# A gated recurrence: half B's state products as sums of three bf16 numbers, the x side with stationary weights, r in 64-column products

## The chip, the cores and the metric

The kernel runs on one core of a Trainium2 chip. The metric is device time in microseconds of one execution, as the median of the runs; lower is better. The engines are named as in the profile: PE is TensorE (matmuls; its weight loads are PEld), DVE is VectorE, ACT is ScalarE, POOL is GpSimd, SP is SyncE, whose queue issues most DMAs.

## What is computed

```python
xT = jnp.swapaxes(x, 0, 1)               # x: (8, 512, 512) = batch, time, units
def step(h, x_t):
    fused = jax.nn.sigmoid(jnp.concatenate([x_t, h], axis=-1) @ w_W + w_b)
    hidden_state, output_state = jnp.split(fused, 2, axis=-1)
    memory_state = x_t @ wx_W + wx_b + hidden_state * (h @ wh_W + wh_b)
    h_new = output_state * h + (1.0 - output_state) * jnp.tanh(memory_state)
    return (h_new, h_new)
_, hs = jax.lax.scan(step, h0, xT)
return x + jnp.swapaxes(hs, 0, 1)
```

There are 512 steps, each of which needs the state h (8 rows of 512 units) that the step before left. All numbers are fp32. In the kernel's names, r is `hidden_state`, z is `output_state`, "hh" (the h of the code's `turn_h`) is `h @ wh_W + wh_b`. The products with x_t (the x side) depend on no state and can be made ahead; those with h are on the recurrence.

## The kernel before

The 512 units are split in four quarters of 128. The state lies transposed, units on partitions: quarters 0 and 1 are half A (tiles `hTA`), 2 and 3 half B (`hTB`). A product takes a quarter of the state as the stationary operand (128 x 32: 8 columns of this step, the rest left from others) and 128 columns of a weight matrix as the moving one. Four such products, one for each j, write to the four column groups of 32 PSUM partitions (`mm` with `32 * j`, lines 177 and 273 to 275).

A group of `GS` = 4 steps shares its PSUM banks: R (r, all units), G (hh and z of half A) and H (z and hh of half B), two of each. The x side of a group is made one group ahead into a bank `xp` (`prefill`, lines 215 to 225: 384 moving columns, one quarter of x in each step), on top of a bias that ScalarE puts there (`seed`); ScalarE copies its parts into R, G and H (`spread`), so that the state's products add to them. VectorE transposes the x part of the tanh's argument (`turn_x`).

The order of PE's work is written out by hand (line 27), followed by one quarter of the x side:

```python
ORDER = "R0 R1 G0 G1 R2 R3 G2 G3 H0 H1 H2 H3"
```

R0 to G1 need half A of the new state; R2 to G3 need half B; so do H2 and H3. All engines run their instructions in the order of the program (`manual_schedule`, line 170), and that is, in a step (lines 351 to 372):

- `turn_r(0)`, `turn_r(1)`: VectorE transposes R's two halves (line 303), ScalarE takes the sigmoid (line 205).
- `turn_h(0)`, `turn_z(0)`: VectorE transposes hh and z of half A out of G (lines 321, 303), ScalarE takes the sigmoid of -z.
- `memory(0)`: a scan on VectorE makes r * hh + x side (lines 283, 342), ScalarE the tanh. `update(0)`: a scan makes the new state of half A (line 347).
- The same for half B out of H; its scans are in two pieces, one for each quarter.
- ScalarE copies both halves of the state into another slot; then `turn_x`, `spread` or `seed`, and three small memsets on VectorE.

GpSimd adds x to the new state (line 385) and the sync queue stores 16 steps at a time (line 395) and loads x two to three blocks ahead (line 101).

Of the kernel before, what the change touches and what calls it, by code (L numbers as in the profile page):

```python
# [10 lines left out]
ALU = mybir.AluOpType  # L11
PSUM = bass.MemoryType.PSUM
# [3 lines left out]
GS = 4  # L16
B = 8
HU = 64

DVE_FILL = 23
IDLE = 3
LAST = 4
SYNC = mybir.DependencyInfo(mybir.DependencyClass.Sync, mybir.DependencyReason.DATA)

ORDER = "R0 R1 G0 G1 R2 R3 G2 G3 H0 H1 H2 H3"

FIRST = "Q0 x Q1 x Q2 x Q3 H0 H1 H2 H3"

BANKS = ("R", "G", "H")

XP = {"G": slice(0, 128), "R": slice(128, 256), "X": slice(256, 384), "H": slice(384, 512)}
# [3 lines left out]
def tile_cond_rnn_residual(  # L37
# [5 lines left out]
    wgr_d: bass.AP,  # L43
    whh_d: bass.AP,
    wh3_d: bass.AP,
    bias_d: bass.AP,
    out: bass.AP,
# [8 lines left out]

# [3 lines left out]
    NG = T // GS  # L80
# [6 lines left out]

    xins = {}


    NX = NQ * TC * B // 2
    head = const.tile([P, NX + NQ * B], F32, name="head")
    nc.scalar.dma_start(out=head, in_=xh)
    hin = head[:, NX:].rearrange("p (k b) -> p k b", k=NQ)

    def load_x(c, half=slice(0, 2)):

        if c < NCH:
            if c not in xins:
                xins[c] = xin_p.tile([P, 2, NQ, TC * B // 2], F32, tag="xin", name=f"xin_{c}")  # L100
            nc.sync.dma_start(
                out=xins[c][:, half], in_=x[c].rearrange("p (e k n) -> p e k n", e=2, k=NQ)[:, half]
            )

    def x_of(c, k, t, n):

        e, t = divmod(t, TC // 2)
        if c == 0 and e == 0:
            first = head[:, :NX].rearrange("p (k n) -> p k n", k=NQ)
            return first[:, k, t * B : (t + n) * B]  # L110
        return xins[c][:, e, k, t * B : (t + n) * B]


    rows4 = const.tile([P, 512], F32, name="rows4")
    nc.vector.memset(rows4, 0.0)
    nc.scalar.dma_start(out=rows4[0:128:32], in_=bias_d)

    wx = const.tile([P, NQ, NQ, 384], F32, name="wx")
    for k in range(NQ):
        nc.sync.dma_start(out=wx[:, k], in_=wx_d[k])  # L120

    wgr = const.tile([P, NQ, NQ, 256], F32, name="wgr")
    for k in range(NQ):
        nc.sync.dma_start(out=wgr[:, k], in_=wgr_d[k])  # L124
    whh = const.tile([P, NQ, NQ, 128], F32, name="whh")
    nc.sync.dma_start(out=whh[:, :3], in_=whh_d)
    nc.sync.dma_start(out=whh[:, 3], in_=wh3_d)

    def wh(bank, k, j):
        return whh[:, k, j] if bank == "H" else wgr[:, k, j, {"G": slice(0, 128), "R": slice(128, 256), "Q": slice(0, 256)}[bank]]  # L130

    load_x(0, 1)

    def pair(n, name, rows, slots):

        if n == "A":
            return const.tile([P, rows, 2, slots], F32, name=name)
        return const.tile([P, 2, rows, slots], F32, name=name).rearrange("p c n s -> p n c s")

    NH = 2 * GS
    hT = [[pair(n, f"hT{n}{i}", 32, 3) for i in range(NH)] for n in "AB"]

    md0 = [[pair(n, f"md0{n}{i}", 32, 2) for i in range(2)] for n in "AB"]
    md1 = [[pair(n, f"md1{n}{i}", 32, 2) for i in range(2)] for n in "AB"]
    hd0 = [[pair(n, f"hd0{n}{i}", B, 3) for i in range(2)] for n in "AB"]
    zeros = const.tile([P, 512], F32, name="zeros")
    nc.vector.memset(zeros, 0.0)
    none = const.tile([P, 128], BF16, name="none")  # L150
    nc.vector.memset(none, 0.0)

    ones = const.tile([P, NQ, 32], F32, name="ones")
    nc.vector.memset(ones, 0.0)
    for j in range(NQ):
        nc.vector.memset(ones[32 * j : 32 * j + 1, j], 1.0)

    nc.scalar.activation(const.tile([P, 1], F32, name="table"), zeros[:, :1], AF.Sigmoid)
    for n, t_ in enumerate(hd0[0] + hd0[1] + md0[0] + md0[1] + hT[0] + hT[1]):
        (nc.vector if n < DVE_FILL else nc.gpsimd).memset(t_, 0.0)  # L160
    for t_ in hd0[0] + hd0[1]:
        nc.gpsimd.memset(t_[:, :, :, 1], -1.0)
    idle = const.tile([P, IDLE], F32, name="idle")

    def state(hf, i, slot=2):

        s = i % GS
        return hT[hf][i % NH][:, B * s : B * s + B, :, slot]

    ctx.enter_context(tc.manual_schedule())  # L170
    banks = [
        {n: psum.tile([P, 128], F32, name=f"{n}{q}") for n in BANKS}
        for q in range(2)
    ]
    xps = [psum.tile([P, 512], F32, name=f"xp{q}") for q in range(2)]

    def mm(out_, lhsT, rhs, start=False):
        nc.tensor.matmul(  # L178
            out_, lhsT, rhs, start=start, stop=False, skip_group_check=True
        )  # L180


    for t_ in list(banks[0].values()) + list(banks[1].values()):
        mm(t_, none[:, :128], none, start=True)
    def warm():

        mm(xps[1], zeros[:, :128], zeros)

    mm(xps[1], zeros[:, :128], zeros, start=True)
    warm()  # L190
    mm(xps[0], ones.rearrange("p j m -> p (j m)"), rows4, start=True)
    bias = const.tile([P, 512], F32, name="bias")
    nc.vector.tensor_copy(bias, xps[0])
    for hf in range(2):
        for slot in (0, 2):
            nc.vector.tensor_copy(
                state(hf, 0, slot), hin[:, 2 * hf : 2 * hf + 2].rearrange("p c b -> p b c")
            )

    written = {}

    def act(key, out_, in_, func, **kw):
        inst = nc.scalar.activation(out_, in_, func, **kw).ins  # L205
        if key in written:
            tc.declare_no_dep(inst, written[key], reason="ordered through VectorE")
        written[key] = inst
        return inst

    def seed(g):

        nc.scalar.copy(xps[g % 2], bias)

    def prefill(g):

        c, t0 = divmod(g * GS, TC)
        for k in range(NQ):
            for j in range(NQ):
                mm(  # L220
                    xps[g % 2][32 * j : 32 * j + 32, 64:448],
                    x_of(c, k, t0, GS),
                    wx[:, k, j, :],
                )
            yield

    def spread(g, names):

        for n in names:
            nc.scalar.copy(banks[g % 2][n], xps[g % 2][:, XP[n]])  # L230

    def turn_x(g, e):

        c0 = XP["X"].start + 32 * e
        nc.vector.transpose(
            md1[e // 2][g % 2][:, :, e % 2, 1], xps[g % 2][:, c0 : c0 + 32]
        )

    def take(it, n=None):
        while n is None or n > 0:  # L240
            if next(it, it) is it:
                return
            n = None if n is None else n - 1

    def x_side():
        for g in range(1, NG):
            yield from prefill(g)

    seed(1)
    take(prefill(0))  # L250
    warm()
    later = x_side()
    spread(0, "RGH")
    for e in range(NQ):
        turn_x(0, e)

    pool_done = {}
    for i in range(T):
        g, s = divmod(i, GS)
        c, t = divmod(i, TC)  # L260
        ps = banks[g % 2]
        if t == 0 and c > 0:
            load_x(c + 3)
        if t == 0:
            ot = out_p.tile([P, TC, NQ, B], F32, tag="ot", name=f"ot_{c}")

        for n in (ORDER if i else FIRST).split():
            if n == "x":
                take(later, 1)
                continue  # L270
            bank, k = n[0], int(n[1])
            hs = hT[k // 2][i % NH][:, :, k % 2, 2]
            for j in range(NQ):
                to = xps[0][:, :256] if bank == "Q" else ps[bank]
                mm(to[32 * j : 32 * j + 32, :], hs, wh(bank, k, j))
        take(later, 1)

        rows = slice(B * s, B * s + B)

        def scans(hf, out_, d0, d1):  # L280

            for c_ in [slice(0, 2)] if hf == 0 else [slice(0, 1), slice(1, 2)]:
                nc.vector.tensor_tensor_scan(  # L283
                    *[t_[:, :, c_].rearrange("p n c s -> p (n c s)") for t_ in (out_, d0, d1)],
                    0.0,
                    ALU.mult,
                    ALU.add,
                )
                yield c_

        if i:
            pg, pr = ps["G"], ps["R"]
        else:
            pg, pr = (xps[0][:, XP[n]] for n in "GR")
        raw = {
            "h": (pg[:, :HU], ps["H"][:, HU:]),
            "z": (pg[:, HU:], ps["H"][:, :HU]),
            "r": (pr[:, :HU], pr[:, HU:]),
        }

        def turned(n, hf):
            t_ = work.tile([P, 2, 32], F32, tag=f"t{n}{hf}", name=f"t{n}{hf}_{i}")
            inst = nc.vector.transpose(t_.rearrange("p c n -> p (c n)"), raw[n][hf]).ins  # L303
            return t_[:, :, rows], inst

        r_done = [None, None]

        def turn_r(hf):
            tr, inst = turned("r", hf)

            if hf == 1 and i + 1 - NH in pool_done:
# [170 lines left out]
```

## Time and profile before

| What | us |
|---|---|
| median of 3 runs (lowest, highest) | 1693.87 (1693.63, 1693.88) |
| span of the profiled execution | 1691.7 |
| what lies around the span, by the median | 2.2 |
| PE busy, DVE busy, ACT busy, POOL busy | 1680.3, 1087.0, 915.5, 231.2 |
| granted TensorE clock, mean | 1.000 |

The span runs from the first to the last instruction. In the groups, a line gives the line of the code, the engine, the operation, what it writes and reads, partitions x elements, how often, its busy time and the mean length of one, then the idle time ahead of it and what ended that. A matmul in fp32 appears as two instructions, each with a weight load. A matmul's end is modelled and includes the way through the array, so lengths of matmuls overlap; the chain shows by how much the next one is later. In the timeline, lines give start, length, engine and what ran, with the wait before it in brackets.

### The profile page before, as it was taken

The numbers are of one execution on the slowest core, as the hardware profiler recorded it, in microseconds if no ns is written. First come the engines' busy times: TensorE is split into PE (matmuls) and PEld (weight loads), VectorE is DVE, ScalarE is ACT, GpSimd is POOL, SyncE is SP. The second block draws the span as 40 slices with busy tenths as digits, with TensorE's granted clock in tenths as the row PEclk, the third lists the DMA queues.
The fourth block names the chain that finished last, engine by engine and source line by source line (L and its number), as shares of the span: only waits on it lengthen the run. The fifth ranks groups of instructions, "written<-read, shape, count | busy, mean of one in ns | idle before, by whom it ended". The sixth has DMA issues, their size and how long they took to land.

```text
span 1691.7 us, 121258 instructions
## 1 busy us (share of the span) xinstructions
PE 1680.3 (99%) x53230; PEld 1467.6 (87%) x53230; DVE 1087.0 (64%) x8229; ACT 915.5 (54%) x5121; POOL 231.2 (14%) x1032
## 2 busy tenths in 40 slices
PE   8999999999999999999999999999999999999998
PEld 6888888888888888888888888888888888888887
DVE  5666666666666666666666666666666666666666
ACT  3555555555555555555555555555555555555554
POOL 0111111111111111111111111111111111111111
PEclk9999999999999999999999999999999999999999
DMA  4000000000000000000000000000000000000000
GB/s 177 17 17 5 17 17 17 17 4 17 17 17 17 4 17 17 17 17 13 9 18 17 17 17 4 17 17 17 17 5 17 17 17 17 4 17 11 11 11 10
DMA packets 11483, 30.86 MB, mean 18 GB/s; under 512 B 1220, under 2 KB 1732, under 8 KB 10952
## 3 DMA queue, kind: packets, MB, share of 16 engines
q1 hardware_dynamic: 10800, 22.94, 3.9%
q8 instruction: 416, 6.82, 1.7%
q14 instruction: 115, 0.94, 0.2%
q10 hardware_dynamic: 152, 0.16, 0.0%
HBM read 14.70 MB, written 8.39 MB: 14 GB/s over the span
## 4 chain that ended last, share of the span: by engine, by line
PE 98%; DMA 1%; DVE 0%; ACT 0%; issue 0%; SPq 0%
PE R L178 26%; PE G L178 26%; PE H L178 26%; PE xp L178 19%; DMA whh<-in_whh_dram 1%; DMA head<-in_xh_dram 0%; DVE md1A L321 0%; DVE hTA L283 0%; ACT hd0A L205 0%; ACT hTA L205 0%; SPq L124 0%; DVE tz L303 0%; ACT hTB L205 0%; DVE hTB L283 0%; ACT hd0B L205 0%
## 5 line engine op out<-in xcount | busy, mean ns | idle before, releaser
L178 PE MATMUL xp<-wx,xin 128*32 128x384 f32 x4032 | 431.3, 486 | 0.0
L178 PEld LDWEIGHTS R<-wgr,hTA 128*32 128x32 f32 x8176 | 247.4, 135 | 206.8 <-DVE hTA L283 206.4
L303 DVE STREAM_TRANSPOSE tr<-R 128x64 f32<-128x64 f32 x1022 | 194.4, 229 | 309.1 <-PE R L178 309.1
L178 PE MATMUL R<-wgr,hTA 128*32 128x128 f32 x8176 | 330.9, 273 | 2.2 <-DVE hTA L283 2.2
L178 PE MATMUL H<-whh,hTA 128*32 128x128 f32 x8192 | 331.3, 273 | 0.8 <-DMA whh<-in_whh_dram 0.8
L178 PE MATMUL H<-whh,hTB 128*32 128x128 f32 x8192 | 331.2, 273 | 0.0
L178 PE MATMUL R<-wgr,hTB 128*32 128x128 f32 x8176 | 330.6, 273 | 0.0
L178 PE MATMUL G<-wgr,hTB 128*32 128x128 f32 x8176 | 330.6, 273 | 0.0
L178 PE MATMUL G<-wgr,hTA 128*32 128x128 f32 x8176 | 330.6, 273 | 0.0
L385 POOL TENSOR_TENSOR ot<-xin,hTB 128x16 f32<-128x16 f32 x503 | 126.4, 251 | 1415.6 <-DVE hTB L283 1324.0
L205 ACT ACTIVATE hd0B<-tz 128x16 f32<-128x16 f32 x512 | 114.9, 224 | 305.3 <-DVE tz L303 305.3
L205 ACT ACTIVATE md0A<-tr 128x16 f32<-128x16 f32 x512 | 119.6, 234 | 265.2 <-DVE tr L303 265.2
L178 PEld LDWEIGHTS H<-whh,hTA 128*32 128x32 f32 x8192 | 260.2, 136 | 1.2 <-DMA whh<-in_whh_dram 1.2
L178 PEld LDWEIGHTS G<-wgr,hTA 128*32 128x32 f32 x8176 | 259.8, 136 | 0.0
L178 PEld LDWEIGHTS H<-whh,hTB 128*32 128x32 f32 x8192 | 254.5, 122 | 0.0
L178 PEld LDWEIGHTS G<-wgr,hTB 128*32 128x32 f32 x8176 | 254.1, 122 | 0.0
L178 PEld LDWEIGHTS R<-wgr,hTB 128*32 128x32 f32 x8176 | 245.2, 122 | 0.0
L283 DVE TENSOR_TENSOR_SCAN hTA<-hd0A,hTA 128x48 f32<-128x48 f32 x512 | 132.1, 258 | 149.2 <-ACT hTA L205 149.2
L283 DVE TENSOR_TENSOR_SCAN hTB<-hd0B,hTB 128x24 f32<-128x24 f32 x1024 | 158.1, 196 | 104.0 <-ACT hTB L205 104.0
L205 ACT ACTIVATE hd0A<-tz 128x16 f32<-128x16 f32 x512 | 118.9, 232 | 111.4 <-DVE tz L303 111.4
L321 DVE STREAM_TRANSPOSE md1A<-G 128x64 f32<-128x64 f32 x511 | 156.8, 307 | 28.7
L205 ACT ACTIVATE hTB<-hTB 128x16 f32<-128x16 f32 x512 | 121.2, 237 | 81.1 <-DVE hTB L283 80.5
(62 smaller groups left out, 1680.2 us busy)
## 6 DMA issues: line engine op xcount, KB each, us to landing
xin<-in_x_dram SPq DMA_DIRECT2D x31, 256.0 KB, 3.8
out_dram<-ot SPq DMA_DIRECT2D x31, 256.0 KB, 3.3
wx<-in_wx_dram SPq DMA_DIRECT2D x4, 768.0 KB, 7.2
wgr<-in_wgr_dram SPq DMA_DIRECT2D x4, 512.0 KB, 9.7
whh<-in_whh_dram SPq DMA_DIRECT2D x1, 768.0 KB
whh<-in_wh_dram SPq DMA_DIRECT2D x1, 256.0 KB, 11.2
out_dram<-ot SPq DMA_DIRECT2D x1, 192.0 KB, 1.9
head<-in_xh_dram ACTq DMA_DIRECT2D x1, 144.0 KB, 5.2
```

The lines of the kernel that those rows point to most:

```text
L178: nc.tensor.matmul(out_, lhsT, rhs, start=start, stop=False, skip_group_check=True)
L205: inst = nc.scalar.activation(out_, in_, func, **kw).ins
L283: nc.vector.tensor_tensor_scan(*[t_[:, :, c_].rearrange("p n c s -> p (n c s)") for t_ in (out_, d0, d1)], 0.0, ALU.mult, ALU.add,)
L303: inst = nc.vector.transpose(t_.rearrange("p c n -> p (c n)"), raw[n][hf]).ins
L321: nc.vector.transpose(md1[hf][g % 2][:, :, :, 0].rearrange("p n c -> p c n"), raw["h"][hf])
L385: return engine.tensor_tensor(ot[:, t, 2 * hf : 2 * hf + 2, :].rearrange("p c n -> p n c"), x_of(c, slice(2 * hf, 2 * hf + 2), t, 1).rearr ...
```

## The change

- **Half B's hh and z.** Each fp32 number of the state and of the weights is written as an exact sum of three bf16 numbers. The weights' parts are made once at the start (`split_weights`: two ScalarE copies and two VectorE subtractions for each quarter). The state's parts are made in every step by two subtractions on VectorE for each half (`split`); each takes the upper 16 bits of a number as the bf16 part and leaves the rest in the next slot. The 24 stationary columns are 3 parts x 8 rows, so that each of 4 quarters x 3 weight parts x 4 column groups gives one bf16 product of 128 columns, into bank B. The nine part products (3 in columns, 3 in accumulation) are summed by the accumulation in PSUM and by what follows on VectorE: the memory scan runs over 5 slots (3 parts, bias or r, x side) and not 2, and z's slots are summed by a `tensor_reduce`.
- **r** is made in two banks, rA and rB, by fp32 products of 64 columns; hh and z of half A stay in G. The stationary operand has 8 columns, and the banks hold one step.
- **The x side** is made for 8 steps at once: the weights are stationary (128 x 32), x moves (64 columns), so that the results come with units on partitions. ScalarE brings each of 12 regions for 8 steps to SBUF with its bias (`leave`, in place of `seed` and `spread`). GpSimd adds the x side to the transposed r of both halves and to z of half A before the sigmoid (`gate`). Block 0 is made whole ahead of step 0.
- VectorE's order in a step: r of A, hh of A, z of A, memory scan of A, r of B, update of A, hh and z of B, the two subtractions for A, memory scan of B, reduction, update of B, the two subtractions for B. The idle memsets and `turn_x` go.
- The last block is stored in one piece, and its adds are all on GpSimd.

```diff
-ORDER = "R0 R1 G0 G1 R2 R3 G2 G3 H0 H1 H2 H3"
+ORDER = "rA01 G01 rB01 rA23 G23 rB23 B01 B23 x x x x x x"
...
+    def split(hf, i):
+        for part in range(2):
+            V.tensor_tensor(
+                state(hf, i, 2, part + 1), state(hf, i, 2, part), upper(hf, i, part), ALU.subtract
+            )
...
+    def split_weights(k):
+        S.copy(wb3[:, k, 0], halves(wb[:, k]))
+        V.tensor_tensor(rest[:, k], wb[:, k], wb3[:, k, 0], ALU.subtract)
+        S.copy(wb3[:, k, 1], halves(rest[:, k]))
+        V.tensor_tensor(wb3[:, k, 2], rest[:, k], wb3[:, k, 1], ALU.subtract)
...
+    def x_region(n, blk, g, c):
+        ch, t0 = divmod(blk * BS, TC)
+        to = xps[n % 3]
         for k in range(NQ):
             for j in range(NQ):
                 mm(
-                    xps[g % 2][32 * j : 32 * j + 32, 64:448],
-                    x_of(c, k, t0, GS),
-                    wx[:, k, j, :],
+                    to[32 * j : 32 * j + 32],
+                    wx[:, k, GATES.index(g), c, 32 * j : 32 * j + 32],
+                    x_of(ch, k, t0, BS),
+                    start=k == 0,
                 )
...
+    def leave(n, blk, g, c):
...
+        S.activation(to, of, AF.Identity, bias=biases[:, i : i + 1])
...
+    later = x_side()
+    for _ in range(12 * NQ):
+        next(later)
+        leave_all()
+    for k in range(NQ):
+        split_weights(k)
+    pieces = {"rA": ("rA", 0, 64), "rB": ("rB", 64, 64), "G": ("G", 128, 128)}
+    def products(i, name, k):
+        hs = st[k // 2][i % NS]
+        c = k % 2
+        if name == "B":
+            flat = top(hs).rearrange("p q b c s -> p (q b c s)")
+            lhsT = flat[:, 6 * c + 5 : 6 * c + 5 + 12 * 23 + 1 : 12]
+            for part in range(3):
+                for j in range(NQ):
+                    mm(bank["B"][32 * j : 32 * j + 24], lhsT, wb3[:, k, part, j], start=k + part == 0)
+            return
+        n, c0, w = pieces[name]
+        lhsT = hs[:, 0, :, c, 2]
+        for j in range(NQ):
+            mm(bank[n][32 * j : 32 * j + B, :w], lhsT, wf[:, k, j, c0 : c0 + w], start=k == 0)
...
+        def gate(name, hf, of, xs, to, key, **kw):
+            p_ = work.tile([P, 2, B], F32, tag=f"p{name}{hf}", name=f"p{name}{hf}_{i}")
+            G.tensor_tensor(p_, turned(name, hf, of), xs, ALU.add)
+            return act(key, to.rearrange("p b c -> p c b"), p_, AF.Sigmoid, **kw)
...
         turn_r(0)
-        turn_r(1)
-        turn_h(0)
-        turn_z(0)
+        V.transpose(
+            md1a[q][:, B * t : B * t + 32, :, 0].rearrange("p n c -> p c n"), bank["G"][:, :HU]
+        )
+        gate("z", 0, bank["G"][:, HU:], xz[q][:, :, rows], hd0[0][i % 2][:, :, :, 2], ("zc", 0, i % 2), scale=-1.0)
         memory(0)
+        turn_r(1)
         update(0)
-        turn_h(1)
-        turn_z(1)
-        memory(1)
-        update(1)
+        V.transpose(
+            md1b[q][:, rows, :, :4].rearrange("p b c s -> p c s b"), bank["B"][:, :HU]
+        )
+        V.transpose(zb[q][:, t, :, :4].rearrange("p c s b -> p c (s b)"), bank["B"][:, HU:])
+        act(("h", 0, (i + 1) % NS), state(0, i + 1, 0), state(0, i + 1), AF.Copy)
+        split(0, i + 1)
+        memory(1)
+        pz = work.tile([P, 2, B], F32, tag="pzB", name=f"pzB_{i}")
+        V.tensor_reduce(pz, zb[q][:, t].rearrange("p c s b -> p c b s"), AX.X, ALU.add)
+        act(("zc", 1, i % 2), hd0[1][i % 2][:, :, :, 2].rearrange("p b c -> p c b"), pz, AF.Sigmoid, scale=-1.0)
+        update(1)
+        act(("h", 1, (i + 1) % NS), state(1, i + 1, 0), state(1, i + 1), AF.Copy)
+        split(1, i + 1)
+        leave_all()
```

## The prediction

> **What bounds the kernel now.** I read the page first (busy line and chain by engine), then the chain in order of time, then the groups by form, then the timeline of one steady step.
>
> ```profile
> PE 1680.3 (99%) x53230; PEld 1467.6 (87%) x53230; DVE 1087.0 (64%) x8229; ACT 915.5 (54%) x5121; POOL 231.2 (14%) x1032
> ...
> PE 98%; DMA 1%; DVE 0%; ACT 0%; issue 0%; SPq 0%
> ```
>
> TensorE is busy for the whole span and holds 98% of the chain that ended last. Busy matmuls can hide waits, so I went on to the chain in order of time (start, length, what), whose pieces repeat:
>
> ```profile
> 802.12 0.87 PE H L178 x32
> 802.99 0.65 PE xp L178 x8
> 803.64 0.44 PE R L178 x16
> 804.08 0.44 PE G L178 x16
> 804.51 0.44 PE R L178 x16
> 804.95 0.44 PE G L178 x16
> 805.38 0.87 PE H L178 x32
> ```
>
> A step takes 805.38 - 802.12 = 3.26 us, with no wait in it. 512 steps are 1669 us; the other 23 us of the span are loading, the first step and the end. Groups by form (last columns: busy, mean ns of one):
>
> ```profile
> L178 PE MATMUL xp<-wx,xin 128*32 128x384 f32 x4032 | 431.3, 486 | 0.0
> L178 PE MATMUL H<-whh,hTB 128*32 128x128 f32 x8192 | 331.2, 273 | 0.0
> L385 POOL TENSOR_TENSOR ot<-xin,hTB 128x16 f32<-128x16 f32 x503 | 126.4, 251 | 1415.6 <-DVE hTB L283 1324.0 <-issue 83.2 <-DVE idle L383 8.3
> L385 DVE TENSOR_TENSOR ot<-xin,hTB 128x16 f32<-128x16 f32 x1 | 0.2, 189 | 0.0
> ```
>
> An fp32 product is two instructions: 8192 are 512 steps x 2 quarters x 4 column groups x 2. Two lengths give a slope of (486 - 273)/(384 - 128) = 0.83 ns a column and a latency of 166 ns. The H piece has 32 instructions on four column groups side by side, so 0.87/8 = 109 ns for each in its group: 128 x 0.83 plus 2.5 ns. Per pair of weight load and matmul, that is 27 ns of PE.
>
> The timeline shows what hangs on the end of G and must be back in time:
>
> ```profile
> 801.91 0.65 PE L178 MATMUL H<-whh,hTA 128*32 128x128 f32 x16
> ...
> 802.17 0.31 DVE L321 STREAM_TRANSPOSE md1A<-G 128x64 f32<-128x64 f32 x1
> ...
> 802.35 0.21 DVE L303 STREAM_TRANSPOSE tz<-G 128x64 f32<-128x64 f32 x1
> 802.52 0.23 DVE L283 TENSOR_TENSOR_SCAN m<-md0A,md1A 128x32 f32<-128x32 f32 x1
> 802.59 0.23 ACT L205 ACTIVATE hd0A<-tz 128x16 f32<-128x16 f32 x1 [0.22 <-DVE tz L303]
> ...
> 802.78 0.22 ACT L205 ACTIVATE hTA<-m 128x16 f32<-128x16 f32 x1
> ...
> 803.04 0.26 DVE L283 TENSOR_TENSOR_SCAN hTA<-hd0A,hTA 128x48 f32<-128x48 f32 x1 [0.29 <-ACT hTA L205]
> 803.21 0.23 DVE L321 STREAM_TRANSPOSE md1B<-H 128x64 f32<-128x64 f32 x1
> 803.35 0.48 PEld L178 LDWEIGHTS R<-wgr,hTA 128*32 128x32 f32 x16 [0.41 <-DVE hTA L283]
> 803.36 0.21 DVE L303 STREAM_TRANSPOSE tz<-H 128x64 f32<-128x64 f32 x1
> ...
> 803.95 0.31 DVE L283 TENSOR_TENSOR_SCAN hTB<-hd0B,hTB 128x24 f32<-128x24 f32 x2 [0.20 <-ACT hTB L205]
> ```
>
> G leaves the array when H starts (801.91); half A's state is done at 803.30 and its weights load at 803.35, while xp occupies PE to 803.43: slack under 0.1 us. VectorE then goes on, in order, to half B: its first scan half ends at about 804.16, against a start of R's second half at 804.30. So two bounds lie nearly on each other: PE's 3.26 us, and a **loop**: end of G, half A, half B behind it on VectorE, then R and G of half B (0.87), 2.25 + 0.11 + 0.87 = 3.23 us. The second one decides this change.
>
> **PE work of a step, after.** In fp32, a 64-column instruction should take 64 x 0.83 + 2.5 = 56 ns in its group. rA and rB: 8 instructions each in every group, 0.44 each, as much as R had. G: 8 x 109 = 0.87, unchanged. x: 4 x 6 x 2 = 48 instructions, 12 in each group, 0.67 (xp had 0.65). Half B's products: 48 bf16 pairs of 128 columns, 12 in each group. No steady row shows bf16; bounds are 56 ns (one pass where the fp32 pair has two each) and the fp32 row's 109. I take 56: 0.67 against H's 0.87. The sum is 0.88 + 0.87 + 0.67 + 0.67 = 3.09 us: 0.17 less a step, 87 us in all, if PE stayed the bound. This is the gain on paper. The pairs rise from 104 to 192 a step.
>
> **The loop, after.** Its terms, from G off the array at 0:
> - h of half A's transpose starts at 0.26 (801.91 to 802.17), that of z at 0.44 (0.18 later) and ends at 0.65.
> - New: GpSimd adds the x side to z. VectorE to GpSimd is 0.08 (state B ends 800.99, add at 801.07), the add 0.25 (the row above); out of GpSimd no row shows, bounds are the other hops, 0.03 and 0.08; I take 0.05. Sigmoid of z at 1.03. Bounds of the add: 0.20 (spacing of two adds) to 0.35 if it meets VectorE's scans.
> - r of half A goes the same way, but 0.44 earlier: its memory scan starts at about 0.7 and is done before 1.0. Its tanh is queued behind z's sigmoid on ScalarE: 1.16, ends 1.38.
> - Update of A at 1.42 (before: 803.04 - 801.91 = 1.13). PE has rB 0.22 + B 0.67 + x 0.67 = 1.56 of cover; the state is back at 1.42 + 0.26 + 0.06 = 1.74, so PE waits about 0.15 here.
> - Half B follows on VectorE: its two transposes at 1.59 and 1.77, then **two new subtractions** of half A's state ahead of the memory scan in the queue. The second needs the first one's result: 1.90, then 1.90 + 0.19 + 0.035 = 2.12, by the 189 ns row. Bound below: 0.11 each, without the write tail.
> - Memory scan of B at 2.23, with 80 elements. Scans of 32 and 48 took 225 and 258 ns, 2.06 a step, so 0.32, and 0.25 before the next can start (the next starts 0.08 before its forerunner's end, as 803.04 + 0.26 to 803.21). Bounds 0.26 and 0.40.
> - New: the reduction of z at 2.48. No row has one; between a transpose of 64 (207 ns) and a scan of 48 (258) I take 0.24, bounds 0.18 and 0.30. Sigmoid at 2.75, update of B at 3.01, done at 3.27. It was at 804.16 - 801.91 = 2.25.
> - PE: weights and start 0.08, then rA23 0.22 and G23 0.44, where R and G took 0.87.
>
> The loop is 3.27 + 0.08 + 0.66 = **4.0 us**, 0.9 above PE's work: the ending wait is rA23 for half B's update. With all low bounds 3.65, with all high ones 4.2. The gain of 0.17 on PE goes into idle time ahead of rA23.
>
> What lies beside the loop: ScalarE's x-side copies (1.5 a step, at most the 265 ns of a 128x128 copy, behind half B's copy, read a block later); the residual adds on GpSimd, done before r's add comes; the second pair of subtractions, behind update(1), wanted by B23 1.2 us later. Their cover is PE's rA23, G23, rB23 and B01; without it, 0.4 us. The seeds, spreads and x-side transposes that go were off the path. The DMAs are the same weights and blocks, minus the split of the last store.
>
> **Ends.** Before, the first step's transposes start at 17.55. After, block 0's whole x side comes first (12 regions x 0.45 = 5.3 us from the last wx chunk's products at 11.44), then four weight splits on ScalarE and VectorE (rows of 128x512: copy 591 ns, VectorE copy 692), 2 us each: half A starts at about 26. The last store is one of 256 KB (3.3 us) and not of 64 KB: with GpSimd's add ahead, some 1.7 longer. So the span is 25.7 + 511 x 4.0 + 3.3 + 4.6 = 2078 us; the timed median stands 2.2 above the span: **2080 us**. A row of 0.1 us in the loop is 51 us.
>
> **Rivals.**
> - **TensorE's instruction rate becomes the bound.** 192 pairs in 4.0 us are 20.8 ns each. This trace never sustains more than one per 27 ns, though its array work alone explains that. Only at the start, out of a queue filled during a wait, eight weight loads of 106 ns fit into 0.16 us (at 8.65), some 7 ns apart. From 20.8 ns a pair up the rate decides; at 27.2 a step takes 5.2 us and the run 2700. (The Trainium skill, TensorE: Matmul & The Clock Gate, section "Wait — 56ns, not 53.3ns?", speaks against the change: matmul starts are never closer than about 25 ns however small. Read for all column groups together it makes 4.8 us a step and about 2490 us; read for each group it costs nothing. No run here shows which.) 17%.
> - **The other side: the loop is covered and PE is the bound.** Then 512 x 3.09 and some 35 us of ends give about 1620 us. It needs the loop under 3.09 to 3.2 us, thus 0.8 less than summed; even all low bounds give 3.65. For it speaks only that the A side's cover is nearly full. 3%, and 1% within 0.2%.
> - **A shorter loop**: two new terms overlap in a way I don't see; 3.3 to 3.65 us, 1730 to 1900 us. 4%.
> - That the change doesn't do what it says is excluded by the instruction order: 48 bf16 pairs, 6 x calls, 5 adds on GpSimd stand in each step.
>
> **Numbers.** The loop case holds 75%, 1906 to 2180 us. To leave out no more than 2 in 10, the range reaches a little into the rate case: 1900 to 2330. About 0.2% is what a measurement of this kernel can tell from no change: faster 0.03, same 0.01, slower 0.96.
>
> **What would show it.** Right: TensorE's largest wait is rA for half B's state, about 0.8 us a step; VectorE's chain holds most of the span; half B's memory scan starts 0.8 us after update A. Wrong, by the rate: no wait ahead of rA23 while x and B products run longer than 0.67. Wrong otherwise: bf16 pieces at 109 ns (inside the cover, little time), or a granted clock below 1.0 in the gaps.

## The result and the profile after

The changed kernel takes 2818.19 us (median of 4 runs, 2812.20 to 2823.31), against 1693.82 for the kernel before on the same chip: a ratio of 1.6637 [1.6614, 1.6661]. The direction was right. The time is 738 us above the forecast of 2080 and lies outside the range.

The page of the changed kernel: the span, the busy line, the queue that brings instructions, and the chain by engine.

```profile
span 2821.3 us, 215844 instructions
...
PE 1853.4 (66%) x98312; PEld 1641.3 (58%) x98312; DVE 1500.9 (53%) x7706; ACT 1014.7 (36%) x4874; POOL 601.3 (21%) x2582
...
q8 instruction: 768, 12.58, 1.8%
...
PE 55%; issue 33%; DVE 8%; ACT 3%; DMA 0%; POOL 0%; DVEq 0%; SPq 0%; POOLq 0%
```

No engine is busy for more than 66% of the span. The loop through VectorE and ScalarE, which I had made the bound, holds 11% of the chain. What stands out is "issue 33%": time in which an engine on the chain waited for nothing that the profile shows. The groups by form tell which engine that is (last columns: idle time ahead of the group, and what ended it):

```profile
L151 PE MATMUL G<-wf,stB 128*8 128x128 f32 x8192 | 400.3, 274 | 118.4 <-issue 118.4
...
L151 PE MATMUL B<-wb,stB 128*24 128x128 bf16 x12288 | 346.9, 221 | 198.6 <-issue 196.1 <-ACT wb L186 1.7 <-DVE wb L187 0.8
...
L151 PE MATMUL rA<-wf,stA 128*8 128x64 f32 x8192 | 266.7, 220 | 214.3 <-issue 206.6 <-DVE stA L307 4.9
...
L151 PE MATMUL rA<-wf,stB 128*8 128x64 f32 x8192 | 239.6, 220 | 45.7 <-DVE stB L307 45.7
```

The wait for half B's state, which I had put at 0.8 us a step ahead of rA23, is the last line: 45.7 us in all, 0.09 a step. PE's idle time stands instead ahead of G, B and rA, ended by "issue": PE had its operands and its buffer, and no instruction. The chain in order of time shows how these waits lie (start, length, what):

```profile
1401.03 0.61 PE B L151 x42
1401.64 1.30 issue
1402.94 0.28 PE B L151 x3
...
1405.02 0.42 PE rA L151 x16
1405.43 0.42 PE G L151 x13
1405.86 0.56 issue
1406.42 0.24 PE G L151
...
1407.04 0.54 PE B L151 x36
...
1407.71 0.67 PE xp L151 x39
1408.38 0.01 issue
1408.39 0.40 PE rA L151 x13
1408.80 1.38 issue
1410.17 0.23 PE rA L151 x2
```

The gaps fall in the middle of B, of G, of rA, at another place each time. Between them PE is quick: 42 of B's products in 0.61 us, 14.5 ns for each pair of load and matmul on the mean of that piece, 58 ns in its column group. Counting in the timeline the matmuls from the end of the first gap (1402.94) to the start of the next (1405.6) gives 3 + 46 + 1 + 2 + 13 + 1 + 2 + 15 + 16 + 16 + 13 = 128, with as many loads: 256 instructions. Over the whole trace, 702 of PE's instructions start more than 0.9 us after the one before (1.47 on the mean, 1031 us in all), and 602 of these breaks come exactly 256 instructions after the last (55 more come 512 after it).

The DMA view of the stretch from 1400 to 1415 us (40 slices) shows what comes in that rhythm:

```profile
DMA  2000000000100000000010000000002000000000
GB/s 44 0 0 0 0 0 0 0 0 0 44 0 0 0 0 0 0 0 0 0 44 0 0 0 0 0 0 0 0 0 44 0 0 0 0 0 0 0 0 0
DMA packets 4, 0.07 MB, mean 4 GB/s; under 512 B 0, under 2 KB 0, under 8 KB 0
...
q8 instruction: 4, 0.07, 1.8%
```

Four packets of the instruction queue, one every 10 slices (3.75 us), and nothing else. Of such packets the page counts 768, 12.58 MB: 16.4 KB each, 64 B times 256. PE's 2 x 98312 instructions are 768 times 256 and 16 more, so q8 carries PE's instructions alone; the page of before has

```profile
q8 instruction: 416, 6.82, 1.7%
```

as 2 x 53230 / 256 = 416. One packet is due in 2821.3/768 = 3.67 us after, in 1691.7/416 = 4.07 before.

### The profile page after: what moved, and what is told of

Read it like the earlier page. It is cut to its first block, busy times and chain, and to the rows that moved or that the text cites. A ratio compares the mean times of both kernels' runs of the same rounds, so it can differ in the third digit from the quotient of the medians.

```text
span 2821.3 us, 215844 instructions
## 1 busy us (share of the span) xinstructions
PE 1853.4 (66%) x98312; PEld 1641.3 (58%) x98312; DVE 1500.9 (53%) x7706; ACT 1014.7 (36%) x4874; POOL 601.3 (21%) x2582
## 3 DMA queue, kind: packets, MB, share of 16 engines
q8 instruction: 768, 12.58, 1.8%
## 4 chain that ended last, share of the span: by engine, by line
PE 55%; issue 33%; DVE 8%; ACT 3%; DMA 0%; POOL 0%; DVEq 0%; SPq 0%; POOLq 0%
PE G L151 15%; PE B L151 13%; PE rA L151 10%; PE xp L151 9%; PE rB L151 8%; DVE md1B L342 2%; DVE stB L307 2%; DVE stA L165 2%; DVE m L307 2%; ACT stB L192 1%; ACT hd0B L192 1%; DVE zb L345 0%; DMA wx<-in_wx_dram 0%; DVE stA L307 0%; DVE md1A L326 0%
## 5 line engine op out<-in xcount | busy, mean ns | idle before, releaser
L151 PE MATMUL xp<-xin,wx 128*32 128x64 f32 x24192 | 482.4, 220 | 113.5 <-issue 113.5
L151 PEld LDWEIGHTS xp<-xin,wx 128*32 128x32 f32 x24192 | 414.7, 110 | 137.9 <-issue 137.9
L151 PE MATMUL G<-wf,stB 128*8 128x128 f32 x8192 | 400.3, 274 | 118.4 <-issue 118.4
L151 PE MATMUL B<-wb,stB 128*24 128x128 bf16 x12288 | 346.9, 221 | 198.6 <-issue 196.1
L151 PE MATMUL G<-wf,stA 128*8 128x128 f32 x8192 | 367.3, 274 | 142.1 <-issue 142.1
L151 PE MATMUL rA<-wf,stA 128*8 128x64 f32 x8192 | 266.7, 220 | 214.3 <-issue 206.6
L151 PEld LDWEIGHTS <-stB 128*24 128x24 bf16 x12288 | 271.6, 122 | 211.8 <-issue 211.8
L151 PE MATMUL rB<-wf,stB 128*8 128x64 f32 x8192 | 275.6, 220 | 114.5 <-issue 114.5
L151 PE MATMUL B<-wb,stA 128*24 128x128 bf16 x12288 | 318.2, 220 | 1.4 <-ACT wb L186 0.5
L151 PE MATMUL rA<-wf,stB 128*8 128x64 f32 x8192 | 239.6, 220 | 45.7 <-DVE stB L307 45.7
L151 PEld LDWEIGHTS <-stA 128*24 128x24 bf16 x12288 | 260.9, 121 | 1.9 <-issue 1.9
```

What stands on the lines that cost most here:

```text
L151: nc.tensor.matmul(out_, lhsT, rhs, start=start, stop=False, skip_group_check=True)
```

## The experiments

The changed kernel's trace leaves three theories. **F**: PE's instructions arrive in chunks of 256, one every 3.55 to 3.75 us, and from there on their number is the time: 384 a step are 1.5 chunks, 5.48 us at 3.65, and 512 of these are 2803 us. **The array (A)**: the products themselves take longer than I took, or each has a price of its own. **The loop (L)**: the way through VectorE, GpSimd and ScalarE is longer than summed. They differ in what the time follows: the number of PE's instructions, their kinds and columns, or neither.

### Instructions added to the kernel before

In e1, e2 and e8 the kernel before gets 8, 24 and 48 products of zeros a step, one column each, added to bank H. They change no result and no other engine's work.

```diff
+        for u in range(24):
+            j = u % NQ
+            mm(ps["H"][32 * j : 32 * j + 32, :1], none[:, :32], none[:, :1])
```

> The kernel before with 8 matmuls of one bf16 column added to each step (zeros times zeros, added into H right after H's products): 104 pairs of weight load and matmul become 112, thus 224 instructions. Theory F (TensorE's instructions arrive in chunks of 256, one per 3.55 to 3.65 us): 224/256 x 3.6 = 3.15 us a step, under the 3.26 that the array needs, so no change beyond the tiny products themselves, 1694 to 1720. Rival S (the skill's floor of 25 ns a matmul start, for all column groups together, added to what the array does): 8 x 25 ns a step, about 1795. Rival P (the stall belongs to the kind of products after the change, not to their number): 1694 to 1720.

Measured: 1724.56 us, 1.0181 [1.0164, 1.0198]. That is 60 ns a step for two products in each group, at most 30 ns each. 224 instructions are 0.875 chunks, 3.26 us at 3.73, and the array's step is 3.26 without the added products: this run does not tell the two apart. It lies 5 us above the range of F and P (1720), far under S's 1795.

> The kernel before with 24 such one-column matmuls a step: 256 instructions a step. Theory F: one chunk a step, 3.55 to 3.65 us instead of 3.26, so 1840 to 1900, with idle time of TensorE put down to issue after each 256 instructions. Rival S: 24 x 25 ns = 0.6 us a step, 2000. Rival P: 1700 to 1740, only the tiny products' own time.

Measured: 1929.48 us, 1.1390 [1.1366, 1.1414], a step of 3.73 us. Six products of 30 ns in a group would make it 3.44 for the array alone. P's 1700 to 1740 and S's 2000 both miss it. F had the sign and the place and was 30 us low, as a chunk here takes 3.73 and not 3.55 to 3.65. The page and the chain of this run:

```profile
PE 1882.5 (98%) x65518; PEld 1652.3 (86%) x65518; DVE 1122.7 (58%) x8229; ACT 918.1 (48%) x5121; POOL 231.4 (12%) x1032
...
q8 instruction: 511, 8.37, 1.9%
...
PE 97%; issue 2%; DMA 1%; DVE 0%; ACT 0%
```

```profile
805.30 0.44 PE G L178 x12
805.74 0.44 PE R L178 x12
806.17 0.04 issue
806.21 0.66 PE G L178 x16
```

PE is 98% busy and holds 97% of the chain, and yet the arrival sets the time. One chunk is a step here, its boundary falls nearly always at the same place, and the wait of some 0.2 us hides in the modelled ends of the matmuls: the last line has G's 16 instructions at 0.66 us where before's chain has 0.44.

> The kernel before with 48 one-column bf16 products of zeros a step (12 in each column group), 208 + 2*48 = 304 instructions a step. Theory F (instructions come in chunks of 256, one per 3.65 to 3.75 us): 304/256 of that = 4.33 to 4.45 us a step, 2240 to 2305 us. Rival, the array alone: 12 products in a group at 30 ns add 0.36 us to the step of 3.26, 3.62 us, 1877 us.

Measured: 2283.86 us, 1.3477 [1.3455, 1.3500], 4.41 us a step: F. In the timeline 41 tiny products start within 0.44 us, 44 ns apart in a group; even at that price 12 of them would make the step 3.8 us. With 304 instructions the boundary moves through the step, and the wait comes into view:

```profile
q8 instruction: 607, 9.95, 1.9%
...
PE 89%; issue 9%; DMA 1%; DVE 0%; ACT 0%; SPq 0%
```

### Instructions taken from the changed kernel

e3 multiplies the state's parts with the first part of the weights only; it leaves out the products with the second and third parts, 64 instructions a step.

```diff
-            for part in range(3):
+            for part in range(1):
```

> The kernel after, half B's products with the first of the three weight parts alone (it leaves out two thirds of these products, so hh and z of half B are made with weights cut to bf16): 192 pairs a step become 160, thus 320 instructions. Theory F: 320/256 x 3.6 = 4.5 us a step, 2290 to 2370. Rival L (the 5.5 us are the loop through VectorE, longer than predicted): these products lie in the loop's cover, so no change, 2800 to 2820. Rival A (PE's array work is what is larger than summed, bf16 at 109 ns a product): 8 x 55 to 109 ns less a step in each group, 2370 to 2600.

Measured: 2417.36 us, 1.4270 [1.4249, 1.4292], 4.65 us a step. A loop longer than summed would have left the time where it was; A's range of 2370 to 2600 holds it too, and e9 is what separates A from F. F's number is low by 2%, again by the chunk's 3.73 (the median distance of two q8 packets in this trace).

e9 computes everything and takes 64 instructions from another place: r in one product of 128 columns, with as many columns in all (the diff cut to its core, as for e10).

```diff
-ORDER = "rA01 G01 rB01 rA23 G23 rB23 B01 B23 x x x x x x"
+ORDER = "r01 G01 r23 G23 B01 B23 x x x x x x"
...
-    pieces = {"rA": ("rA", 0, 64), "rB": ("rB", 64, 64), "G": ("G", 128, 128)}
+    pieces = {"r": ("r", 0, 128), "G": ("G", 128, 128)}
```

> The changed kernel with r in one 128-column fp32 product instead of two of 64 columns, the rest unchanged: 384 - 64 = 320 instructions a step, as many as in e3 but of other kinds, and with the array's own work unchanged (as many columns). Theory F: 320/256 of 3.65 to 3.74 us = 4.56 to 4.68 us a step, 2360 to 2420 us. Rival, the array's columns decide: no change, 2818 us. Rival, three parts of the bf16 products decide: no change either.

Measured: 2413.33 us, 1.4253 [1.4232, 1.4274], within 0.2% of e3. The busy lines of the two pages, e3's and e9's:

```profile
PE 1603.4 (66%) x81928; PEld 1419.5 (59%) x81928; DVE 1490.5 (62%) x7706; ACT 1020.7 (42%) x4874; POOL 605.9 (25%) x2582
...
q8 instruction: 640, 10.49, 1.9%
```

```profile
PE 1836.1 (76%) x81926; PEld 1597.9 (66%) x81926; DVE 1489.2 (62%) x7706; ACT 1028.0 (43%) x4874; POOL 603.0 (25%) x2582
...
q8 instruction: 640, 10.49, 1.9%
```

PE's work differs by 233 us of busy time, the count and the time are the same. This is what excludes the array.

e10 also computes everything: x in blocks of 16 steps, half as many products of twice the columns.

```diff
-BS = 8
+BS = 16
...
-ORDER = "rA01 G01 rB01 rA23 G23 rB23 B01 B23 x x x x x x"
+ORDER = "rA01 G01 rB01 rA23 G23 rB23 B01 B23 x x x"
```

> The changed kernel with x products in 16-step blocks of twice the columns instead of 8-step blocks, the rest unchanged: 384 - 48 = 336 instructions a step. Theory F: 336/256 of 3.65 to 3.74 us = 4.79 to 4.91 us a step, 2475 to 2545 us with a start some 5 us longer. Rival, the array's columns decide: no change, 2818 us, as the columns of x are as many as before.

Measured: 2529.76 us, 1.4936 [1.4913, 1.4958]: F, with the columns unchanged.

### The loop by itself

e4 leaves out two thirds of the weights' parts, as e3, and the x products of all blocks after the first (the copies out of PSUM stay). 224 instructions a step need 3.3 us, so the loop should show.

```diff
-            for j in range(NQ):
+            for j in range(NQ if blk == 0 else 0):
```

> As the one before, and the x side's matmuls left out behind block 0 (the copies that fetch its results stay, and find block 0's values): 224 instructions a step. Theory F: 3.15 us for the instructions, which no longer bounds; what remains is the loop through VectorE, predicted at 4.0 us a step, thus 2080 (by the prediction's bounds 1906 to 2182), with TensorE waiting ahead of rA for half B's state. If the loop is longer than the prediction's sum this run says by how much. Rival L: 2800.

Measured: 2139.10 us, 1.2630 [1.2611, 1.2649]. Now the chain is as I had forecast it for the change itself:

```profile
DVE 40%; ACT 22%; PE 14%; issue 11%; POOL 11%; DVEq 1%; POOLq 1%; DMA 0%; SPq 0%
```

and the timeline repeats after 4.08 us (800.95 to 805.03, update of half A):

```profile
800.95 0.26 DVE L307 TENSOR_TENSOR_SCAN stA<-hd0A,stA 128x48 f32<-128x48 f32 x1 [0.35 <-ACT stA L192]
...
801.27 0.21 DVE L345 STREAM_TRANSPOSE zb<-B 128x64 f32<-128x64 f32 x1
...
801.40 0.38 DVE L165 TENSOR_TENSOR stA<-stA 128x16 f32<-128x16 f32 x2
...
801.70 0.32 DVE L307 TENSOR_TENSOR_SCAN m<-md0B,md1B 128x80 f32<-128x80 f32 x1
...
801.93 0.28 DVE L350 TENSOR_REDUCE pzB<-zb 128x16 f32<-128x80 f32 x1
...
802.57 0.26 DVE L307 TENSOR_TENSOR_SCAN stB<-hd0B,stB 128x48 f32<-128x48 f32 x1 [0.36 <-ACT hd0B L192]
...
802.88 0.42 PE L151 MATMUL rA<-wf,stB 128*8 128x64 f32 x16 [0.55 <-DVE stB L307]
...
803.55 0.41 PE L151 MATMUL rB<-wf,stB 128*8 128x64 f32 x16
...
803.98 0.21 DVE L287 STREAM_TRANSPOSE tz<-G 128x64 f32<-128x64 f32 x1
...
804.33 0.24 POOL L293 TENSOR_TENSOR pz<-tz,xz 128x16 f32<-128x16 f32 x1 [0.34 <-ACT md0A L192]
804.60 0.23 ACT L192 ACTIVATE hd0A<-pz 128x16 f32<-128x16 f32 x1 [0.35 <-POOL pz L293]
804.73 0.21 ACT L192 ACTIVATE stA<-m 128x16 f32<-128x16 f32 x1
...
805.03 0.26 DVE L307 TENSOR_TENSOR_SCAN stA<-hd0A,stA 128x48 f32<-128x48 f32 x1 [0.35 <-ACT stA L192]
```

From G off the array (803.55): sigmoid of z at 1.05 (forecast 1.03), tanh's start at 1.18 (1.16), update of half A at 1.48 (1.42); from there half B's memory scan 0.75 later (0.81), its update 1.62 later (1.59), rA 1.93 later (1.93). The forecast loop of 4.0 us measures 4.08 in this step. Over the whole run, from one update of half A to the next, the mean is 4.11.

e5 is e4 with half A's two subtractions behind the reduction, in VectorE's order.

```diff
-        split(0, i + 1)
         memory(1)
         pz = work.tile([P, 2, B], F32, tag="pzB", name=f"pzB_{i}")
         V.tensor_reduce(pz, zb[q][:, t].rearrange("p c s b -> p c b s"), AX.X, ALU.add)
+        split(0, i + 1)
```

> The kernel with one weight part and without the later x products (224 instructions a step, computation left out as there), and half A's two subtractions moved behind the reduction in VectorE's order. Where the instructions no longer bound, the loop does: there the two subtractions held the memory scan of half B from 801.40 to 801.70. Theory L2 (they are a term of the loop, as the prediction had it): 0.30 us a step less, 2139 becomes 1985. Rival: something else (PE, ScalarE's copies) ends the step, 2120 to 2139.

Measured: 2039.69 us, 1.2039 [1.2019, 1.2059]: 0.19 us a step less, not 0.30. The place is confirmed, the size is not. The timeline of this run (VectorE alone):

```profile
801.37 0.26 DVE L307 TENSOR_TENSOR_SCAN stA<-hd0A,stA 128x48 f32<-128x48 f32 x1 [0.35 <-POOL pr L293]
...
801.70 0.21 DVE L345 STREAM_TRANSPOSE zb<-B 128x64 f32<-128x64 f32 x1
801.93 0.33 DVE L307 TENSOR_TENSOR_SCAN m<-md0B,md1B 128x80 f32<-128x80 f32 x1
...
802.81 0.26 DVE L307 TENSOR_TENSOR_SCAN stB<-hd0B,stB 128x48 f32<-128x48 f32 x1
```

Half B's memory scan starts 0.56 us after the update of half A and not 0.75, and the update of half B follows 0.88 after that scan (0.87 in e4). So the whole difference to 0.30 lies ahead of the scan: it starts 0.23 after the transpose before it (801.70 to 801.93), where in e4 the first subtraction started 0.13 after that transpose (801.27 to 801.40). Why the scan comes later there is not shown.

### Everything computed, with fewer instructions

e6 joins e9's and e10's edits: 272 instructions a step. e7 is e6 with e5's order.

> The whole computation of the kernel after with fewer instructions for TensorE: r in one product of 128 columns, the x side in blocks of 16 steps with 128 moving columns. 136 pairs a step instead of 192, 272 instructions, the same columns through the array. Theory F: the chunks allow 272/256 x 3.65 to 3.74 = 3.88 to 3.97 us; the loop, 4.10 as measured without the instruction bound plus 0.22 since r is one piece of 0.44 behind half B's state, is 4.32 and bounds: 2210 to 2290 with a longer start. Rival A (array work or the kind of product bounds after the change): the columns are the same, so 2750 to 2820.

Measured: 2245.07 us, 1.3253 [1.3234, 1.3273], a step of 4.31 us against the loop of 4.32.

> As the one before, with half A's subtractions behind the reduction. Loop 4.32 - 0.30 = 4.02, chunks 3.88 to 3.97: both near each other, 2080 to 2180. If the two bounds lie so near that they add, up to 2230.

Measured: 2152.22 us, 1.2702 [1.2684, 1.2721], a step of 4.13 us: 0.18 less than e6, as e5 gained 0.19 on e4 and not 0.30. Both follow their loops and no longer the arrival; e6's chain:

```profile
DVE 38%; ACT 21%; PE 16%; POOL 14%; issue 10%; DVEq 1%; POOLq 0%; DMA 0%; SPq 0%
```

No version came near before: even where the arrival does not decide, the loop of the changed order is 3.9 us or more, against a step of 3.26.

All runs together, in the order of PE's instructions (the span over q8's packets, both from the pages):

| Run | PE instructions a step | q8 packets | span, us | us per packet | bound |
|---|---|---|---|---|---|
| changed kernel | 384 | 768 | 2821.3 | 3.67 | arrival |
| e10 | 336 | 672 | 2527.5 | 3.76 | arrival |
| e9 | 320 | 640 | 2410.9 | 3.77 | arrival |
| e3 | 320 | 640 | 2414.7 | 3.77 | arrival |
| e8 | 304 | 607 | 2281.9 | 3.76 | arrival |
| e7 | 272 | 544 | 2149.3 | 3.95 | loop |
| e6 | 272 | 544 | 2244.3 | 4.13 | loop |
| e2 | 256 | 511 | 1927.1 | 3.77 | arrival |
| e4 | 226 | 451 | 2137.2 | 4.74 | loop |
| e5 | 226 | 451 | 2039.5 | 4.52 | loop |
| e1 | 224 | 448 | 1722.4 | 3.84 | array or arrival |
| before | 208 | 416 | 1691.7 | 4.07 | array |

Six kernels with quite different work stand at 3.67 to 3.77 us a packet, none stands below, and those above have another bound that the chain shows, but for e1, which does not tell. Why the five others stand some 0.1 above the changed kernel is not shown. (e4 and e5 have 224 instructions in a steady step; block 0's products are in the mean.)

What sets the 3.7 us stays open in part. In the changed kernel's trace a q8 transfer takes 1.04 us, starts 1.14 us after the first instruction of a chunk, and the next chunk runs 1.38 us after it has landed (medians, at the 702 breaks). The three add up to 3.56 us, and the median distance of two packets is 3.55: at these breaks the three follow one another without overlap. So the transfer is the smaller part (the page's 1.8% is a share of 16 DMA engines; the packets are in transfer for 29% of the time). Which of request, transfer or hand-over could be shortened was not tried.

## Why the prediction was wrong, point by point

- **The bound: the step that failed.** I took the loop at 75% and "TensorE's instruction rate becomes the bound" at 17%. It was the rate, by e2, e3, e8, e9 and e10. The profiled execution is 743 us above the forecast span of 2078. From one update of half A to the next, its mean step is 5.45 us, against 4.11 in e4: (5.45 - 4.11) x 511 = 685 us are the arrival above the loop. The loop's own error, (4.11 - 4.0) x 511, is 56, and the ends are the few us that are left.
- **The evidence against the rate was read wrongly.** I had noted that 192 pairs in 4.0 us are 20.8 ns each and that before's trace never sustains less than 27. Against that I set eight weight loads 7 ns apart at the start. These came out of a filled queue: a burst tells how fast the array takes instructions (14.5 ns a pair here), not how fast they are supplied. My "at 27.2 a step takes 5.2 us and the run 2700" was near, with the wrong reason: 27.2 was before's array pace, while the supply gives 3.65/128 = 28.5 ns a pair. The prediction left out the q8 row of before's page: one packet per 4.07 us, where 384 instructions in 4.0 us need one per 2.7. That alone shows no ceiling, but it would have named the resource that the change asks half as much again of.
- **The rule of the skill.** The Trainium skill, TensorE: Matmul & The Clock Gate, section "Wait — 56ns, not 53.3ns?", has starts never closer than about 25 ns. Read for all column groups together it is refuted by 42 pairs in 0.61 us, 14.5 ns; for each group it agrees with e1's 30 ns. Its 2490 us was nearer than my forecast, by accident. The page of the Trainium skill that I should have weighed is another: Runtime: NRT & Kernel Launch, section "Instruction fetch mechanics", says that instructions come in blocks of 16 KiB, 256 instructions each, and that the cost of crossing a boundary is mostly hidden. The blocks agree with q8's 16.4 KB. That the cost is hidden holds for before (4 breaks of over 0.9 us in its trace) and fails here: 702 such breaks, 1031 us.
- **"PE work of a step, after", 3.09 us: right, and without effect.** I took 56 ns for a bf16 or a 64-column fp32 instruction in its group; in the bursts B's and rA's matmuls start 55 to 56 ns apart in theirs. e9 shows why it did not matter.
- **The loop, 4.0 us: right to 3%** (4.11 on the mean, in e4). What was off: update A starts 0.09 us after tanh's end (804.94), where I took 0.04, and z's add 0.14 after its transpose's end (804.19), where I took 0.08. Each of these waits for two engines; that this is the reason is argued, not tested. It is not the other engine's work: in 162 steps of the changed kernel ScalarE's sigmoid of r had ended over 0.2 us before the transpose, and z's add came 0.145 after the transpose all the same (median). The scan of 80 (317 ns in the changed kernel; I took 324) and the reduction (272; I took 240) were near. Of the new subtractions, 0.19 us a step can be moved out of the way (e5).
- **The ends: right in sum.** Span minus 511 mean steps is 39 us in the changed kernel and in e4, where I had summed 33.6. The first transposes start some 6 us later than the 25.7 I took (32.14 in the changed kernel); the end is about 1 us shorter.
- **What would show it.** "Wrong, by the rate: no wait ahead of rA23" came out, 0.09 us a step of it left. The other half of that test, x and B products longer than 0.67, was wrongly put: the bursts keep their pace and the waits fall anywhere.
- **The other rivals.** "The loop is covered and PE is the bound" (1620) and "a shorter loop" (1730 to 1900) are excluded by e4's 4.11 us, without any arrival in the way.

## What to carry to other kernels

Count the bounding engine's instructions in a step and price their arrival as a resource of its own: here one packet of 256 TensorE instructions took 3.67 to 3.77 us, about 29 ns for a pair of load and matmul, and the page's instruction queue row divided by the span shows how near a kernel is to it (before: 4.07). Splitting products into more and smaller ones, or fp32 into bf16 parts, spends this resource even where it saves columns. And "issue" on a chain whose waits fall at a different instruction each time, a fixed number of instructions apart, is the mark of it; where a step holds a whole number of packets it hid in longer matmuls (e2), and the packet count told.

## What the runs showed that I had not expected

- PE at 98% busy and 97% of the chain can be waiting for instructions (e2): the array's work was at most 3.44 us of a step of 3.73.
- The kernel before had little room. By the pace of the runs here, 3.67 to 3.76 us, its 416 packets are 1527 to 1564 us (an estimate), 8 to 10% below its span; no run shows a faster arrival.
- A one-column product costs at most 30 ns (e1) and in one stretch 44 ns (e8) in its column group, where a 128-column bf16 product costs 56 to 58.
